# Part of a depthwise convolution moved from VectorE to TensorE, four rows to a product in four column tiles

## The chip, the cores and the metric

The kernel runs on one core of a Trainium2 chip. The metric is the device time of the whole program in microseconds (us); before the change its median over three runs is 2747.23 us (2745.68 to 2749.08). The engines are called as in the profile: PE is TensorE's matmul, PEld its weight load, DVE VectorE, ACT ScalarE, POOL GpSimd, SP SyncE (it issues transfers only).

## The reference

The input is x, 4 images of 384 channels of 48 x 48 float32. For each image:

```python
x_flat = x.reshape(B, C, N).transpose(0, 2, 1)              # N = 48*48 = 2304 tokens
local = conv(x, conv_w, 7x7, padding='SAME', groups=C)      # depthwise: each channel by itself
local = local * inv + (bn_beta - bn_mean * inv)             # batch norm, inv = gamma*rsqrt(var+eps)
x_norm = layernorm(x_flat)                                  # over the 384 channels
q, k, v = x_norm @ qkv_w.T + qkv_b                          # 8 heads of 48
q = q + layernorm(local_flat)                               # the convolution joins the query
out = softmax(q @ k.T * 48**-0.5) @ v
return x_flat + (out @ proj_w.T + proj_b)                   # back to NCHW
```

The convolution has 49 taps a channel, and every output token needs it before its query is whole.

## The kernel before

**Tiling.** The 384 channels lie as CC = 3 chunks of 128 partitions, in an order that packs head pairs. An image's tokens are cut in two ways. For layer norm, keys and values there are NG = 6 groups of 384 tokens (8 image rows), g = 0 to 5. For the convolution, queries and attention there are NA = 5 groups a image, of ROWS = 8, 10, 10, 10, 10 image rows, so 384 or 480 tokens; over the four images they are numbered t = 0 to 19.

**The convolution.** `load_slab` brings a group's rows with three rows above and below into a slab, on the POOL queue. `conv_ops(t)` is a generator that yields one tap of one chunk at a time: one DVE instruction (L331) that multiplies the shifted window of the slab by the tap's weight (`cw`, one per channel) and adds it to `accs[t]`. The weights contain the batch norm's factor, and the first tap adds its shift: for t = 0 on DVE (L327), for all later groups on ACT in `first_taps` (L295). `taps` are sorted by the distance of their row, then of their column, from the middle. All generators are chained into one `stream`; `convolve_first(n)` takes n taps of it in the start stage, `convolve(point)` a planned number later.

**What TensorE does of it.** Only ten taps (`PE_TAPS`) of chunk 0 of group t = 0: `make_diagonals` builds ten diagonal matrices on ACT (L340), `products` multiplies the shifted windows by them into one PSUM bank (L347), and `add_products` adds that bank to the accumulator on DVE (L1088). The order of t = 0 is therefore: chunks 1 and 2 tap by tap in turn, and then the 39 left taps of chunk 0 alone.

**The start stage** (0 to 159 us) normalizes image 0 and makes its keys and values, group by group, in an order written out by hand for each engine. `from_x(0, g)` is a generator of pairs of projections, `both(making)` runs one pair: its products on PE and then its evacuations on ACT. For a group g the order is: values 0 and 1; the mean of the next group's x (`mean_by_chunk`, three products of 128 x 384 against a matrix of 1/384; a float32 product is two PE instructions); 7 taps; `centre` on DVE (L536) and squares on ACT; value 2 and key 0; 6 taps; the sum of squares over the three chunks (two DVE adds, `sum_squares`, L493 and L494) and its mean (`mean_in_place`, one product, L526); keys 1 and 2; the root on ACT; the first key's low half (`lows_out`, L731); queries 0 and 1; 9 taps; two more low halves; two DVE steps of Newton and the scaling of the next x (L616); query 2; 7 taps. The values of group g + 1 need that scaled x. For g = 5 the group's convolved rows t = 0 are normalized in place of a next x, and become queries (`local_end`, `query_end`, `low_queries`).

**Attention.** A group t has twelve slots, s = 0 to 11 (four head pairs, three batches of six blocks of 128 keys). A slot is 36 score products (L1032), six exponentials on ACT (L1040) and 24 instructions of weighing (L1047). Beside them DVE does taps and the norm of the next group: `norm.sum` of its accumulator (L493, L494), `mean_of_sum`, `centre`, squares, `mean_kept`, root, `local_end`, `query_end`, `low_queries`. In t = 0 these stand at slots 8 to 10. `low_queries` makes the queries' low half on DVE (L900) and then moves rows within SBUF by six transfers (L905, L907), three on SP and three on another queue; the first scores need all of them.

**Between images** a stage with points ("kv", t, g, h) makes the next image's keys and values and the last image's output projection; its residual sums are `finish` (L1013), which free the PSUM bank they read.

**The planner.** `spare` and `spare_at_keys` give, in us, the DVE time that is free at each point, less the costs of what else is done there; `due` says by which point each group's convolution must be whole; `plan` spreads the taps over the points at the least rate that meets all due points, and `share` holds the result.

Of the kernel before, what the change touches and what calls it, by code (L numbers as in the profile page):

```python
# [10 lines left out]
F32 = mybir.dt.float32  # L11
HALF = mybir.dt.float32r
AF = mybir.ActivationFunctionType
# [15 lines left out]
X_LATER = 3  # L29
OUT_SLOT = 7  # L30
WARM = 14
PE_TAPS = 10
AHEAD = 18
FIRST_ROOM = 4.0

# [13 lines left out]
def unshifted_pass(  # L49
# [40 lines left out]
    def columns_of(t):  # L90
        return size(tokens[t % NA])
# [14 lines left out]
    def two_banks(name="r"):  # L106
        return ps.tile([P, 2, 512], F32, tag="r", name=name)
# [121 lines left out]
    def pack():  # L229
# [18 lines left out]
    diagonals = [  # L248
        work.tile([P, 2, GM], F32, tag="pt", name="pt", bufs=4) for _ in range(-(-PE_TAPS // 6))
    ]  # L250
    staged = [
        work.tile([P, CC, GM], F32, tag="qs", name="staged", bufs=5)[:, :, :C] for _ in range(3)
# [48 lines left out]
    def conv_ops(t):  # L301
        b, g = divmod(t, NA)
        if t + 1 < NT:
            load_slab(*divmod(t + 1, NA))
        slab, first, end = slabs[b, g]
        if t == 0:
            begin_sums(t)
            nc.vector.memset(accs[0][:, 0, :], 0.0)
        while soon:
            soon.popleft()()  # L310
        acc = accs[t]

        order = [(tap, c) for tap in taps for c in range(CC)]
        if t == 0:
            order = [o for o in order if o[1]] + [(tap, 0) for tap in taps[PE_TAPS:]]
        for i, (tap, c) in enumerate(order):
            if i == len(order) - AHEAD and t + 1 < NT:
                begin_sums(t + 1)
                soon.append(lambda: first_taps(t + 1))
            part = window(slab, acc[:, c, :], g, first, end, c, tap)  # L320
            if not part:
                continue
            src, dst = part
            weight = cw[:, c, tap : tap + 1]
            if tap == taps[0]:
                if t == 0:
                    nc.vector.tensor_scalar(  # L327
                        dst, src, weight, shift[:, c : c + 1], ALU.mult, ALU.add
                    )
            else:  # L330
                nc.vector.scalar_tensor_tensor(dst, src, weight, dst, ALU.mult, ALU.add)  # L331
            if t == 0 or tap != taps[0]:
                yield

    def diagonal(i):
        return diagonals[i // 6].rearrange("p i f -> p (i f)")[:, i % 6 * P : i % 6 * P + P]

    def make_diagonals():
        for i in range(PE_TAPS):
            nc.scalar.mul(diagonal(i), ident, cw[:, 0, taps[i] : taps[i] + 1])  # L340

    def products():
        total = two_banks()[:, 0, : columns_of(0)]
        slab, first, end = slabs[0, 0]
        for i, tap in enumerate(taps[:PE_TAPS]):
            src, part = window(slab, total, 0, first, end, 0, tap)
            nc.tensor.matmul(  # L347
                part, lhsT=diagonal(i), rhs=src, start=i == 0, stop=i == PE_TAPS - 1
            )
        return total  # L350

# [65 lines left out]
    weights = [0.0]  # L417
    for t in range(1, NT):
        last = ("slot", t - 1, norm_slots(t - 1)[0] - (t >= NA), t < NA) if t % NA else ("kv", t, 4, 0)
        counts.append(t * (each - CC))  # L420
# [665 lines left out]
    def add_products():  # L1086
        a = accs[0][:, 0, :]
        nc.vector.scalar_tensor_tensor(a, first_sum, shift[:, 0:1], a, ALU.add, ALU.add)  # L1088


    def warm(n):
        m = two_banks()[:, 0, 0:P]
# [51 lines left out]
    norm.scale(norm.newton())  # L1144
    both(making)
    convolve_first(7)
    for g in range(1, NG):

        last = g == NG - 1
        making = from_x(0, g)  # L1150
        both(making)
        if last:
            added = output_bias()
        else:
            norm = Norm(xn[0, g + 1])
            norm.mean_by_chunk(norm.src)
            convolve_first(7)
        if g in (3, 5):
            keep_stack(0, g // 2 - 1)
        norm.centre()  # L1160
        norm.squares()
        if last:
            convolve_first(6)
        both(making)
        if last:
            norm.mean_by_chunk(norm.buf)
        else:
            convolve_first(6)
            norm.sum_squares()
            both(making)  # L1170
            norm.mean_in_place()
        norm.root()
        if last:
            convolve_first(9)
            local_end(0, norm.newton())
            query_end(0, True)
            both(making)
            low_queries(0, 0, nc.scalar)
            convolve_first(2)
            lows_out(1)  # L1180
            both(making)
            convolve_first(4)
            both(making)
            continue
        lows_out(1)
        both(making)
        convolve_first(9)
        lows_out(2)
        norm.scale(norm.newton())
        both(making)  # L1190
        if g == NG - 2:
            assert n_first >= each - PE_TAPS
# [5 lines left out]
    made = n_first - (each - PE_TAPS)  # L1198
    plan(made)
    convolve("start")  # L1200

    for t in range(NT):
        b, g = divmod(t, NA)
        if g == 0 and b:
# [4 lines left out]
            for gk in range(NG):  # L1209
# [727 lines left out]
```

## Time and profile before

| what | value |
|---|---|
| median of three runs | 2747.23 us |
| the profiled execution | 2748.89 us |
| its span, first to last instruction | 2747.0 us |
| mean granted TensorE clock | 0.997 |
| convolution on DVE (L331), 2871 instructions | 1685.9 us busy |
| scores (L1032) and weighing (L1047) on PE | 969.9 and 1167.5 us busy |
| projections and means on PE (L621), groups of w_qk, w_v and w_o | 283.7, 147.0 and 85.2 us busy |
| start stage, to the first score | 158.88 us |
| attention of t = 0, first score to first score of t = 1 | 158.88 to 259.31 us |

The shares of busy time say that PE is nearly always busy, but a matmul's end is modelled, so they do not say that it runs at its pace. The pace is read from the starts: equal slots follow each other at 9.07 us with 480 tokens and at 7.38 us with 384, and a slot that takes longer has lost time. The busy times by 20 us (us from the span's start, then each engine's busy time and number of instructions, granted clock, DMA share, GB/s) show where PE has gaps:

```profile
core 0: us, PE busy (x) PEld busy (x) DVE busy (x) ACT busy (x) POOL busy (x), PEclk, DMA share, GB/s
100.00:120.00 20.00, 17.59 (x50) 9.79 (x49) 18.98 (x35) 8.47 (x16) 12.32 (x25) 0.91 0.36 79
200.00:220.00 20.00, 18.75 (x144) 11.18 (x144) 20.00 (x34) 14.02 (x21) 1.45 (x2) 1.00 0.46 141
220.00:240.00 20.00, 17.12 (x128) 10.27 (x125) 19.97 (x33) 11.80 (x18) 4.38 (x7) 1.00 0.74 184
```

In these stretches PE has gaps while DVE has almost none, and in the first the granted clock falls as well.

### The profile page before, as it was taken

The numbers are of one execution on the slowest core, as the hardware profiler recorded it, in microseconds if no ns is written. First come the engines' busy times: TensorE is split into PE (matmuls) and PEld (weight loads), VectorE is DVE, ScalarE is ACT, GpSimd is POOL, SyncE is SP. The second block draws the span as 40 slices with busy tenths as digits, with TensorE's granted clock in tenths as the row PEclk, the third lists the DMA queues.
The fourth block names the chain that finished last, engine by engine and source line by source line (L and its number), as shares of the span: only waits on it lengthen the run. The fifth ranks groups of instructions, "written<-read, shape, count | busy, mean of one in ns | idle before, by whom it ended". The sixth has DMA issues, their size and how long they took to land.

```text
span 2747.0 us, 45879 instructions
## 1 busy us (share of the span) xinstructions
PE 2718.1 (99%) x16358; PEld 1538.0 (56%) x16358; DVE 2334.3 (85%) x4065; ACT 1672.2 (61%) x2319; POOL 600.4 (22%) x1073
## 2 busy tenths in 40 slices
PE   8999999999999999999999999999999999999999
PEld 5565555555565655555555655555555565555555
DVE  7999999989898999988889999889788888986212
ACT  4356777777335767777622667777752376766662
POOL 4541101112453111011155211111225501110110
PEclk9999999999999999999999999999999999999999
DMA  7454544446355445354555553545635545444442
GB/s 142 96 151 116 137 120 127 132 129 182 99 151 154 134 132 137 122 148 124 149 137 135 163 154 107 140 127 142 148 108 159 144 138 133 138 132 126 143 144 76
DMA packets 159710, 369.10 MB, mean 134 GB/s; under 512 B 58416, under 2 KB 107600, under 8 KB 159472
## 3 DMA queue, kind: packets, MB, share of 16 engines
q0 software_dynamic: 71232, 278.45, 35.2%
q1 hardware_dynamic: 82496, 77.13, 12.4%
q10 hardware_dynamic: 5744, 10.50, 1.2%
q8 instruction: 132, 2.16, 0.3%
q14 instruction: 106, 0.87, 0.1%
HBM read 258.14 MB, written 64.14 MB: 117 GB/s over the span
## 4 chain that ended last, share of the span: by engine, by line
PE 82%; DVE 12%; DMA 4%; issue 1%; ACT 1%; SPq 0%; POOL 0%; DVEq 0%; ACTq 0%; POOLq 0%
PE o L1047 39%; PE r L1032 32%; PE r L621 11%; DVE acc L331 7%; DMA four<-parts 1%; DMA parts<-part 1%; DVE k L731 1%; DMA qs<-qs 0%; DVE xr L1013 0%; DMA wide<-k 0%; DVE xn L616 0%; DVE xn L881 0%; DVE acc L869 0%; DMA pb<-in_proj_b_dram 0%; DMA qk_vec<-in_qk_b_dram 0%
## 5 line engine op out<-in xcount | busy, mean ns | idle before, releaser
L331 DVE SCALAR_TENSOR_TENSOR acc<-slab,vec,acc 128x470 f32<-128x470 f32 (+9 forms) x2871 | 1685.9, 657 | 1.3
L1040 ACT ACTIVATE pt<-r 128x960 f32<-128x960 f32 (+1 forms) x1440 | 1248.4, 942 | 248.8 <-PE o L1047 157.2
L1047 PE MATMUL o<-pt,v 128*64 128x480 f32 (+1 forms) x5760 | 1167.5, 555 | 0.4 <-ACT pt L1040 0.4
L1032 PE MATMUL r<-qs,ks 64*128 64x480 f32 (+1 forms) x8640 | 969.9, 374 | 7.6 <-DVE xr L1013 4.1
L1032 PEld LDWEIGHTS r<-qs,ks 64*128 64x128 f32 x8640 | 784.8, 184 | 274.6 <-issue 173.7
L1047 PEld LDWEIGHTS o<-pt,v 128*64 128x64 f32 x5760 | 392.8, 137 | 661.2 <-issue 568.6
L693 POOL DMA_DIRECT2D ks<-wide x220 | 159.8, 726 | 1363.4 <-PE r L1032 1286.3
L621 PE MATMUL r<-xn,w_qk 128*128 128x384 f32 x864 | 283.7, 486 | 0.0
L924 ACT COPY o<-o 113x480 f32<-113x480 f32 (+1 forms) x160 | 87.1, 544 | 286.3 <-PE o L1047 286.2
L621 PEld LDWEIGHTS r<-xn,w_qk 128*128 128x128 f32 x864 | 164.2, 190 | 114.5
L621 PE MATMUL r<-w_v,xn 128*128 128x384 f32 x432 | 147.0, 493 | 3.8 <-DVE xn L616 2.4
L715 ACT COPY v<-r 128x384 f32<-128x384 f32 x72 | 32.1, 480 | 190.7 <-PE r L621 190.7
L943 DVE TENSOR_TENSOR ao<-ao,o 113x480 f32<-113x480 f32 (+1 forms) x120 | 75.8, 632 | 78.8 <-ACT o L924 78.6
L621 PEld LDWEIGHTS r<-w_v,xn 128*128 128x128 f32 x432 | 82.1, 192 | 64.1 <-issue 4.7
L900 DVE TENSOR_TENSOR qs<-xn,qs 128x480 fp32r<-128x480 f32 (+1 forms) x60 | 38.0, 633 | 70.7 <-ACT qs L895 70.7
L678 POOL DMA_DIRECT2D wide<-k x144 | 72.1, 503 | 95.3 <-ACT k L728 82.0
L621 PE MATMUL r<-af,w_o 128*128 128x384 f32 (+1 forms) x270 | 85.2, 470 | 0.0
L943 DVE TENSOR_TENSOR aot<-aot,o 113x480 f32<-113x480 f32 (+1 forms) x40 | 25.3, 632 | 65.0 <-ACT o L924 64.9
L114 POOL DMA_DIRECT2D slab<-in_x_dram x76 | 41.9, 558 | 145.7 <-DVE acc L331 142.4
L745 ACT ACTIVATE xn<-r,qkb 128x384 f32<-128x384 f32 x72 | 39.4, 578 | 55.5 <-PE r L621 40.6
L934 ACT COPY ao<-o 113x480 f32<-113x480 f32 (+1 forms) x60 | 32.6, 543 | 64.5 <-PE o L1047 64.5
L728 ACT ACTIVATE k<-r,qkb 128x384 fp32r<-128x384 f32 x72 | 39.4, 581 | 52.7 <-PE r L621 39.7
(143 smaller groups left out, 1355.5 us busy)
## 6 DMA issues: line engine op xcount, KB each, us to landing
ks<-wide POOLq DMA_DIRECT2D x220, 768.0 KB, 5.0
qs<-qs SPq DMA_DIRECT2D x352, 60.0 KB
slab<-in_x_dram POOLq DMA_DIRECT2D x24, 432.0 KB, 7.5
wide<-k POOLq DMA_DIRECT2D x96, 96.0 KB, 2.3
wide<-ks POOLq DMA_DIRECT2D x12, 768.0 KB, 4.3
xr<-in_x_dram POOLq DMA_DIRECT2D x16, 576.0 KB, 5.3
rb<-rden SPq DMA_DIRECT2D x32, 270.0 KB
held<-ao POOLq DMA_DIRECT2D x12, 720.0 KB, 3.9
```

The lines of the kernel that those rows point to most:

```text
L114: queue.dma_start(out=dst[p0 : p0 + piece.shape[0]], in_=piece)
L331: nc.vector.scalar_tensor_tensor(dst, src, weight, dst, ALU.mult, ALU.add)
L621: nc.tensor.matmul(dst, lhsT=weights(c), rhs=src(c), start=c == 0, stop=c == CC - 1)
L678: nc.gpsimd.dma_start(out=last[16 * u : 16 * u + 16, 0], in_=k[r : r + 16, 0])
L693: queue.dma_start(out=place_keys(b, p, i), in_=wide[b, p][:, :, at])
L728: nc.scalar.activation(k[:, 0, :], r[:, :G], AF.Identity, bias=bias)
L745: nc.scalar.activation(src[:, i, :], q[:, :G], AF.Identity, bias=qkb[:, 0, i : i + 1])
L924: nc.scalar.copy(part[0 : 64 + HA], sums[0 : 64 + HA, 0, :n])
L943: nc.vector.tensor_add(dst, dst, part[0 : 64 + HA])
L1032: nc.tensor.matmul(r[:, j, :n], lhsT=ks[rows, w, at], rhs=qs[rows, m, :], start=i == 0, stop=i == 2,)
L1040: nc.scalar.activation(pt, r[:, :, :n], AF.Exp, scale=SCALE)
L1047: nc.tensor.matmul(sums[halves[j], 0, : columns_of(t)], lhsT=values[t // NA, kb // NB][:, first : first + 64], rhs=pt[:, j, :], start=i == ...
```

## The change

Chunk 0 of the second group (t = 1, 480 tokens) is convolved by TensorE alone; DVE does chunks 1 and 2 of it (96 taps). All three chunks of t = 0 are DVE's, in turn (147 taps); the diagonals and their sum are gone.

- `copies_in` makes four tiles by 16 transfers on SP. Tile q holds the 32 channels of quarter q four times, on partitions 0 to 31, 32 to 63 and so on, each copy shifted by one more image row. A column of such a tile holds four rows of a channel, so one product of 128 rows does four taps of one column offset (dy = 0 to 3); a second one with 96 rows does the other three (dy = 4 to 6, `a` = 1).
- `spread_out` and `taps_out` make the weights: for each quarter, column offset and `a`, a matrix of 128 (or 96) x 32 with the taps of each channel on four (three) small diagonals. Four products choose the quarters' taps, seven ACT copies put them in place, and two DVE multiplies of 128 x 896 and 96 x 896 spread them.
- `products` runs 7 column offsets x 2 x 4 quarters = 56 products into one bank, each quarter in its own column tile of 32 output partitions. One ACT instruction adds the shift and writes the chunk of `accs[1]`.
- The means of the x of groups 2 to 5 are made as one product from the sum of the three chunks, two DVE adds at the end of the group before (`norm.sum`, `mean_in_place`), in place of three products.
- The counts of `convolve_first` change: 22 a group in place of 29 and 24 more in group 2, where `products` stands; 179 taps before attention in place of 183.
- `spare_at_keys` takes 1.5 and 3.0 us off the points (5, 3) and (5, 4); the queries' transfers between images are all put on SP.

```diff
-PE_TAPS = 10
+SHIFTS = 4
...
-        for c in range(CC):
+        for c in range(t == 1, CC):
             src, dst = window(slab, accs[t][:, c, :], g, first, end, c, taps[0])
...
-            begin_sums(t)
-            nc.vector.memset(accs[0][:, 0, :], 0.0)
+            begin_sums(0)
+            begin_sums(1)
...
-        if t == 0:
-            order = [o for o in order if o[1]] + [(tap, 0) for tap in taps[PE_TAPS:]]
+        if t == 1:
+            order = [o for o in order if o[1]]
...
+    def copies_in():
+
+        slab, first, end = slabs[0, 1]
+        slab = slab[:, 0].rearrange("p (h w) -> p h w", w=W)
+        for q, rows in enumerate(quarters):
+            for i, to in enumerate(quarters):
+                n = min(rows_kept, end - first - i)
+                nc.sync.dma_start(out=copy_of(q)[to, 0:n], in_=slab[rows, i : i + n])
...
+    def taps_out():
+        m = two_banks()[:, 0, 0 : 4 * T0].rearrange("p (q v) -> p q v", q=4)
+        for q in range(4):
+            nc.tensor.matmul(
+                m[:, q, :],
+                lhsT=chosen[:, q * P : (q + 1) * P],
+                rhs=cw[:, 0, :],
+                start=True,
+                stop=True,
+            )
+        for i, rows in enumerate(quarters):
+            for a in range(2):
+                dy = a * SHIFTS + i
+                if dy < KS:
+                    nc.scalar.copy(few_taps[rows, a], m[rows, :, dy * KS : (dy + 1) * KS])
+        for a in range(2):
+            k, dst = taps_of(a)
+            w = few_taps[0:k, a].rearrange("p q d -> p (q d)")
+            nc.vector.tensor_tensor(
+                dst[0:k],
+                same_row[0:k].rearrange("p (o j) -> p o j", o=1).to_broadcast([k, 28, 32]),
+                w.rearrange("p (i o) -> p i o", o=1).to_broadcast([k, 28, 32]),
+                ALU.mult,
+            )
 
     def products():
-        total = two_banks()[:, 0, : columns_of(0)]
-        slab, first, end = slabs[0, 0]
-        for i, tap in enumerate(taps[:PE_TAPS]):
-            src, part = window(slab, total, 0, first, end, 0, tap)
-            nc.tensor.matmul(
-                part, lhsT=diagonal(i), rhs=src, start=i == 0, stop=i == PE_TAPS - 1
-            )
-        return total
+        total = two_banks()[:, 0, : columns_of(1)]
+        order = sorted(range(KS), key=lambda d: abs(d - PAD))
+        todo = [(a, d) for d in order for a in range(2)]
+        n = ROWS[1]
+        for a, d in todo:
+            k, w = taps_of(a)
+            dx = d - PAD
+            c0, c1 = max(0, -dx), min(W, W - dx)
+            for q, rows in enumerate(quarters):
+                nc.tensor.matmul(
+                    total[rows].rearrange("p (h w) -> p h w", w=W)[:, :, c0:c1],
+                    lhsT=w[0:k, q * KS + d, :],
+                    rhs=copy_of(q)[0:k, a * SHIFTS : a * SHIFTS + n, c0 + dx : c1 + dx],
+                    start=(a, d) == todo[0],
+                    stop=(a, d) == todo[-1],
+                )
+        nc.scalar.activation(accs[1][:, 0, :], total, AF.Identity, bias=shift[:, 0:1])
...
-            (5, 1): 4.5, (5, 2): 0.6,
+            (5, 1): 4.5, (5, 2): 0.6, (5, 3): 1.5, (5, 4): 3.0,
...
-    make_diagonals()
+    copies_in()
+    spread_out()
...
-    first_sum = products()
...
-    add_products()
...
+    norm = Norm(xn[0, 2])
+    norm.sum()
     for g in range(1, NG):
...
-            norm = Norm(xn[0, g + 1])
-            norm.mean_by_chunk(norm.src)
-            convolve_first(7)
+            norm.mean_in_place()
+            convolve_first(6)
...
-            convolve_first(6)
+            if g == 1:
+                taps_out()
+            if g == 2:
+                products()
+                convolve_first(24)
+            convolve_first(5)
             norm.sum_squares()
...
-        convolve_first(9)
+        convolve_first(6)
...
-        convolve_first(7)
+        convolve_first(5)
+        if g < NG - 2:
+            norm = Norm(xn[0, g + 2])
+            norm.sum()
...
-                    low_queries(t, 0, nc.scalar)
+                    low_queries(t, 0)
```

More of the change, by code (lines that the diff above doesn't have):

```diff
@@ L247, in unshifted_pass @@
     w_o = const.tile([P, CC, C], F32, tag="w_o", name="w_o")
-    diagonals = [
-        work.tile([P, 2, GM], F32, tag="pt", name="pt", bufs=4) for _ in range(-(-PE_TAPS // 6))
+    spread_taps = [
+        work.tile([P, CC, GM], F32, tag="ao", name="spread").rearrange("p c n -> p (c n)")
+        for _ in range(2)
+    ]
+    copies = [
+        work.tile([P, CC, GM], F32, tag="qs", name="copies", bufs=5).rearrange("p c n -> p (c n)")
+        for _ in range(2)
     ]
@@ L313, in conv_ops @@
         order = [(tap, c) for tap in taps for c in range(CC)]
-        if t == 0:
-            order = [o for o in order if o[1]] + [(tap, 0) for tap in taps[PE_TAPS:]]
+        if t == 1:
+            order = [o for o in order if o[1]]
         for i, (tap, c) in enumerate(order):
             if i == len(order) - AHEAD and t + 1 < NT:
-                begin_sums(t + 1)
+                if t:
+                    begin_sums(t + 1)
                 soon.append(lambda: first_taps(t + 1))
@@ L333, in conv_ops @@
                 yield
[L335 to L340, printed above, removed]
-    def products():
-        total = two_banks()[:, 0, : columns_of(0)]
-        slab, first, end = slabs[0, 0]
-        for i, tap in enumerate(taps[:PE_TAPS]):
-            src, part = window(slab, total, 0, first, end, 0, tap)
-            nc.tensor.matmul(
-                part, lhsT=diagonal(i), rhs=src, start=i == 0, stop=i == PE_TAPS - 1
-            )
-        return total
+    quarters = [slice(32 * i, 32 * i + 32) for i in range(4)]
@@ new lines, in unshifted_pass, with copy_of @@
+    few_taps = piece(2, 4, KS)
+    same_row = piece(32)
+    chosen = spread_taps[0][:, 2 * 448 : 2 * 448 + 512]
+    rows_kept = max(ROWS) + SHIFTS
+    def copy_of(q):
+        n = rows_kept * W
+        return copies[q // 2][:, q % 2 * n : (q % 2 + 1) * n].rearrange("p (h w) -> p h w", w=W)
+    def copies_in():
[5 more added lines that the diff above has]
+                nc.sync.dma_start(out=copy_of(q)[to, 0:n], in_=slab[rows, i : i + n])
@@ new lines, in taps_of, with spread_out @@
+    def taps_of(a):
+        k = P - 32 * (a * SHIFTS + SHIFTS - KS)  if a else P
+        return k, spread_taps[a][:, 0:896].rearrange("p (i j) -> p i j", j=32)
+    def spread_out():
+        each_four = chosen.rearrange("p (q i j) -> p q i j", q=4, i=4)
+        nc.scalar.copy(
+            each_four,
+            ident.rearrange("p (q o j) -> p q o j", q=4, o=1).to_broadcast([P, 4, 4, 32]),
+        )
+        nc.vector.tensor_reduce(
+            same_row, ident.rearrange("p (i j) -> p j i", j=32), AX.X, ALU.add
+        )
@@ new lines, in taps_out @@
+    def taps_out():
[21 more added lines that the diff above has]
+                ALU.mult,
+            )
@@ new lines, in products @@
+    def products():
+        total = two_banks()[:, 0, : columns_of(1)]
[13 more added lines that the diff above has]
+                    stop=(a, d) == todo[-1],
+                )
+        nc.scalar.activation(accs[1][:, 0, :], total, AF.Identity, bias=shift[:, 0:1])
@@ L419, in unshifted_pass @@
         last = ("slot", t - 1, norm_slots(t - 1)[0] - (t >= NA), t < NA) if t % NA else ("kv", t, 4, 0)
-        counts.append(t * (each - CC))
+        counts.append(counts[-1] + (each - CC if t > 1 else (CC - 1) * (KS * KS - 1)))
         weights.append(weights[-1] + (counts[-1] - counts[-2]) * columns_of(t) / G)
@@ L1084, in convolve_first @@
             next(stream)
-    def add_products():
-        a = accs[0][:, 0, :]
-        nc.vector.scalar_tensor_tensor(a, first_sum, shift[:, 0:1], a, ALU.add, ALU.add)
     def warm(n):
@@ L1191, in unshifted_pass @@
         if g == NG - 2:
-            assert n_first >= each - PE_TAPS
+            assert n_first >= each
             norm = Norm(accs[0])
             norm.mean_by_chunk(norm.src)
-        convolve_first(7)
+        convolve_first(5)
+        if g < NG - 2:
+            norm = Norm(xn[0, g + 2])
+            norm.sum()
     lows_out(2)
     nc.vector.tensor_add(pb, pb, added)
-    made = n_first - (each - PE_TAPS)
+    made = n_first - each
     plan(made)
```

## The prediction

> **What bounds the kernel now.** I read the page first (busy shares, then the chain that ended last), then who TensorE (PE) waited for over the whole span, then the timeline around each of those waits.
>
> ```profile
> PE 2718.1 (99%) x16358; PEld 1538.0 (56%) x16358; DVE 2334.3 (85%) x4065; ACT 1672.2 (61%) x2319; POOL 600.4 (22%) x1073
> ...
> PE 82%; DVE 12%; DMA 4%; issue 1%; ACT 1%; SPq 0%; POOL 0%; DVEq 0%; ACTq 0%; POOLq 0%
> ```
>
> PE bounds the span; VectorE (DVE) owns 12% of the chain. So a change can gain in two ways: fewer PE instructions, or DVE earlier where PE waits for it. PE's own waits, in total us, times, longest:
>
> ```profile
> PE r L1032 <- DVE xr L1013: 4.1, 2, 2.1
> ...
> PE r L621 <- ACT sq L488: 2.9, 1, 2.9
> PE r L621 <- DVE xn L616: 2.4, 1, 2.4
> ```
>
> Each starts with DVE being late. The timeline shows that each costs more than its wait. Prices in the start stage (start, us, line, shape, count):
>
> ```profile
> 23.10 2.33 PE L795 MATMUL r<-staged,of_ln 128*1 128x384 f32 x18 [1.74 <-issue]
> 29.34 6.29 PE L347 MATMUL r<-slab,pt 128*128 128x384 f32 x20
> 74.33 2.10 PE L621 MATMUL r<-xn,mean_w 128*128 128x384 f32 x6
> 113.02 5.83 PE L621 MATMUL r<-w_v,xn 128*128 128x384 f32 x12 [2.41 <-DVE xn L616]
> ```
>
> A float32 product is two instructions. Groups 1, 2 and 3 start their values at 50.46, 70.46 and 90.45: 20.0 us for 62 instructions of 384 columns, 0.3225 us each. The twelve at 113.02, after PE had sat idle 2.41 us, took 0.49 each: half clock for a while, another 2 us. L795 is the row most like the new products: three column tiles (output partitions 0, 32, 64), 18 instructions whose starts lie between 23.1 and 25.0. One after the other they would need 18 x 0.3225 = 5.8 us; in 2.33 us all three tiles must have run at once.
>
> DVE's taps:
>
> ```profile
> 20.71 14.08 DVE L331 SCALAR_TENSOR_TENSOR acc<-slab,vec,acc 128x376 f32<-128x376 f32 x28
> 89.41 8.43 DVE L331 SCALAR_TENSOR_TENSOR acc<-slab,vec,acc 128x360 f32<-128x360 f32 x14
> ```
>
> 28 taps that alternate between two chunks take 0.50 each. From 89.92 to 118.5 DVE works off the leftover taps of chunk 0 alone, each adding to what the one before wrote: 14 take 0.60 each, though their windows are no larger. A step in the critical chain at 90.51 reads 0.62.
>
> The first attention group (t=0) and an image boundary:
>
> ```profile
> 206.07 3.04 PE L1032 MATMUL r<-qs,ks 64*128 64x384 f32 x31 [1.25 <-DMA qs<-qs]
> ...
> 236.90 1.65 DVE L536 TENSOR_TENSOR acc<-acc,sq 128x1440 f32<-128x1440 f32 x1
> ...
> 239.24 4.21 PE L621 MATMUL r<-sq,mean_w 128*128 128x480 f32 x6 [2.88 <-ACT sq L488]
> ```
> ```profile
> 845.32 3.76 DVE L331 SCALAR_TENSOR_TENSOR acc<-slab,vec,acc 128x450 f32<-128x450 f32 x6
> ...
> 849.00 1.34 DVE L1013 SCALAR_TENSOR_TENSOR xr<-r,pb,xr 128x480 f32<-128x480 f32 x2
> ...
> 850.39 1.61 PE L1032 MATMUL r<-qs,ks 64*128 64x384 f32 x12 [2.01 <-DVE xr L1013]
> ...
> 851.92 5.42 PE L1047 MATMUL o<-pt,v 128*64 128x384 f32 x24
> ```
>
> An undisturbed slot of 384 columns lasts 7.38 us (scores start at 167.14, 174.51, 181.90). Against that, slot 6 of t=0 is 1.65 late (204.03 to 213.06), and slots 9 and 10 start 14.47 apart (228.91, 243.38) where slot and mean need 7.38 + 2.42: 4.7 lost. At the boundary six taps of point ("kv", 5, 5, 4) stand ahead of the two residual sums that free a PSUM bank; the slot lasts 11.42, so 4.0 are lost. The same point costs 3.9 at 2178.56 and 0.5 at 1513.56.
>
> [...]
>
> **The change, part by part.**
>
> *PE, start stage.* Gone: 20 instructions of L347, 6.3 us, and 4 of 6 instructions in four first means, 16 x 0.3225 = 5.2. New: 14 tap steps x 4 tiles x 2 = 112 instructions. With four tiles at once that is 28 steps; the windows average 463 of 480 columns, 0.3225 x 463/384 = 0.389, so 10.9, and 0.5 to fill: 11.4. Bounds: 10.9 below; 43.6 if no tiles overlap. I take 11.4 because L795 shows three whole tiles at once. The four selecting products of taps_out are 8 instructions of 49 columns; pack (L234) took 1.66 for 14, so 1.0. Net +0.9.
>
> *DVE, start stage.* Taps before attention fall from 183 to 179. All three chunks of the first group now alternate: 147 taps at a mean of 0.467 by their windows are 68.6. Before, 98 at that price and 39 dependent at 0.575 were 68.2: ten more taps for nothing. Of the second group 32 taps stand where 46 did: 14 x 0.61 = 8.5 less. Memset and add_products: 0.9 less. Added: eight adds of first sums at 0.59 (L493 and L494 cost that) = 4.7; two multiplies of 128x896, about 1.05 each by L536's 1.35 for 1152; the identity's sum 0.3. Net about -2.
>
> *Order decides what that is worth.* Without L347, PE reaches the mean of xn 1 about 6 us sooner, but the centring waits behind 31 taps on DVE; that chain gains only the 1.9 us in which DVE idled at 36.67 and add_products, and PE idles some 3 us, with half clock likely. Group 1 starts 1 to 3 us earlier; I take 2. In group 1 the two multiplies stand on DVE right after the centring, and need PE (the values, then the selecting products) and seven small ACT copies (0.2 each, by L861 and L810): DVE waits about 3 us, with five taps, the sum of squares and the key's low half queued behind it, and PE's next mean waits for that sum. Group 2 then starts 1.9 later than before. Group 2 takes 58 x 0.3225 + 11.4 = 30.1 on PE; its 24 extra taps (11 to 13 us) lie beside the products: +11.9 at its end. Groups 3 and 4 have 58 instructions, 18.7 us each, and DVE (22 taps at 0.43 and 8 us of norm work, 17.7) no longer falls behind, so the stall at 113.02 with its half clock goes. Group 5's values start 4.6 later; but what ended before there was DVE's centring of accs[0] at 140.81, behind 7 taps; with those gone it waits for its mean and starts at about 141.9. The first score is **1.1 us later** (bounds -4 to +6 with four tiles).
>
> *Other engines.* The 16 copies go on SP after w_o: 16 x 0.6 issue, from 39.3 to about 50; the key stacking that began at 39.98 comes up to 10 us later, which nobody reads before attention, and its key buffer returns at about 62. ACT loses ten L340 (3.0) and gains copies: nothing on the path.
>
> *t=0.* Following plan's arithmetic with the new counts, its slots get 123 taps instead of 131; up to the centring at 236.90 seven fewer, 4.3 us. The squares then come just as PE needs them, so PE never idles long enough to lose clock: of 4.7 + 1.65 I expect **-6.0**. Slots 0 and 11, late by their transfers, stay as they are.
>
> *t=1, t=2.* Ten taps fewer in each. The mean at 445.36 waited 0.8, and the slot after 455.41 is 0.8 long by late squares: **-1.3**.
>
> *Boundaries.* The new costs take point (5, 4) from 6 or 5 taps to 0 and (5, 3) from 5 to 3. The residual sums then end before PE wants the bank: 4.0 + 0.5 + 3.9 = -8.4. low_queries puts six transfers on SP instead of three each on SP and ACT: at 840.26, six issues of 0.7 and some 2.2 to land give 846.7, and PE is ready at 845.9; about 0.7, 0 and 0.9 at the three. Net **-6.9**. SP's key stacking moves 2 us later, with 15 us in hand.
>
> *Elsewhere* the taps come back as one or two more per later group; PE keeps its 9.07 us slot there while DVE has room, so nothing.
>
> Sum: 1.1 - 6.0 - 1.3 - 6.9 = -13.1. The profiled execution took 2748.89 (span 2747.0 and 1.9 around it); it lies 1.7 above the median 2747.23. So 2734.
>
> **Rivals.**
> - *The start stage is dearer* (0.20). Three tiles at once give 37 steps, +3.6; two give 56, +10.9; half clock after the idle in group 0 or 1 adds about 2. For: four were never seen, and 8 loads must fit into 0.39 us. Against: L795. Result 2738 to 2745.
> - *The transfers eat the boundaries' gain* (0.08). The transfers issued at 255.99 took 5.3 us to land; with that instead of 2.2 each boundary loses 3 us: 2743. Against: the boundary is not loading keys.
> - *Slower: the column tiles run one after the other* (0.12). 112 x 0.389 = 43.6 instead of 10.9, in group 2, where nothing covers it, for DVE has only 24 taps to do: 2767. It decides from a products stage of 25 us. For: the fourth tile, with changing row counts (128 and 96), is unseen. Against: L795, and the two tiles of L1047 (24 instructions in 4.09, 0.34 per pair).
> - *Better* (0.12): DVE's relief wins in the start stage too, no wait in group 1, no half clock: 4 to 6 us more, 2729.
>
> **How the numbers follow.** The forecast has 0.48: 2734, its own range 2729 to 2739. With the better case, the dearer start and the transfers, 2725 to 2745 leaves out the serial tiles and a little at the edges. A measurement can tell 0.2%, 5.5 us, from no change. Below 2741.7 lie the forecast, the better case, three quarters of the dearer start and a little of the transfers: 0.78. Slower is the serial case, 0.12; the rest 0.10.
>
> **What would show it.** Products of about 11.5 us in group 2; taps of group 3 at 0.47; no wait of PE at L621 in group 4; the first score near 160; slots 9 and 10 of t=0 about 10 apart; boundary slots of 7.4 to 8.3. The forecast is wrong if the products take over 15 us, if PE idles over 2 us twice in groups 0 to 2, or if the slots' stalls stay.

## The result, and the profile after

The changed kernel takes 2740.54 us (median of 14 runs, 2736.99 to 2743.9); the kernel before, run beside it, 2746.26 us (14 runs, 2742.41 to 2750.27). The ratio is 0.9979 (95% interval 0.9971 to 0.9987): 5.7 us faster, where 13.1 were forecast. (The ratios in this document are the recorded ones, from runs side by side; they are not quotients of the medians.)

The profiled execution of the changed kernel took 2736.99 us. It is the fastest of its 14 runs, while the profiled one of the kernel before, 2748.89, lies near the upper end of its own. The two profiles therefore differ by 11.9 us, twice what the medians do. So both kernels were profiled a second time (the first two experiments). The table puts the four executions side by side, in us, by stages that are read from the starts of the score products (the attention of t = 4, 9 and 14 ends 9.07 us after the start of its last slot, and the boundary's row begins there):

| stage | before | before, second | change | change, second | forecast of the difference |
|---|---|---|---|---|---|
| start stage, to the first score | 158.9 | 158.6 | 161.0 | 165.2 | +1.1 |
| t = 0 | 100.4 | 100.6 | 94.6 | 94.6 | -6.0 |
| t = 1 to 4 | 445.2 | 445.5 | 444.0 | 443.8 | -1.3 |
| first boundary, t = 5 to 9 | 669.6 | 668.9 | 667.4 | 668.6 | |
| second boundary, t = 10 to 14 | 664.3 | 664.3 | 663.7 | 663.7 | |
| third boundary, the rest | 708.6 | 707.4 | 704.3 | 704.3 | -6.9 for all three |

The t = 0 to 4 rows are as forecast in both pairs. The start stage and the boundaries are not settled by one pair: the start is 2.2 or 6.7 us longer, the boundaries are 7.0 or 3.9 us shorter.

The page of the changed kernel, busy shares and the chain that ended last:

```profile
PE 2715.1 (99%) x16442; PEld 1536.5 (56%) x16442; DVE 2313.1 (85%) x4036; ACT 1671.0 (61%) x2317; POOL 599.5 (22%) x1073
...
PE 89%; DVE 8%; DMA 2%; ACT 1%; SPq 0%; issue 0%; POOL 0%; DVEq 0%; ACTq 0%
```

Compared with before, DVE has 29 instructions and 21 us less to do, and its share of the chain falls from 12% to 8%. PE has 84 instructions more and yet 3 us less of busy time. What PE waited for (total us, times, longest):

```profile
PE r L593 <- DVE sq L561: 2.7, 1, 2.7
...
PE r L688 <- ACT sq L550: 2.5, 1, 2.5
```

Of the waits shown of before (residual sums, scaled x, squares of slot 9) none is over 0.5 us now. Two new ones stand in the start stage. Its PE timeline (start, us, line, shape, count, idle before and its releaser):

```profile
39.34 2.20 PE L688 MATMUL r<-sq,mean_w 128*128 128x384 f32 x6 [2.48 <-ACT sq L550]
...
63.17 0.88 PE L593 MATMUL r<-sq,mean_w 128*128 128x384 f32 x2 [2.68 <-DVE sq L561]
...
78.78 11.11 PE L410 MATMUL r<-copies,spread 128*32 128x480 f32 x112
...
100.24 4.03 PE L688 MATMUL r<-w_v,xn 128*128 128x384 f32 x12
...
118.95 4.03 PE L688 MATMUL r<-w_v,xn 128*128 128x384 f32 x12
...
137.66 2.10 PE L688 MATMUL r<-acc,mean_w 128*128 128x384 f32 x6
```

The 112 instructions of the products take 11.11 us, 0.397 for each of the 28 steps of four, where one product of their mean length is 0.389 by the prediction's estimate: all four column tiles run at once. Groups 3 and 4 last 18.7 us each, and the stall at 113 is gone. The two waits are the first and the second line: group 0's mean waits for squares, group 1's for a sum that DVE makes late. Why late, DVE's timeline shows:

```profile
57.59 2.09 DVE L393 TENSOR_TENSOR spread<-start_up 128x896 f32<-128x896 f32 x2 [2.98 <-ACT start_up L389]
...
62.47 0.56 DVE L561 TENSOR_TENSOR sq<-sq 128x384 f32<-128x384 f32 x1
```

DVE idles 2.98 us for the weights' ACT copies, and the five taps and the two sums for PE's mean (the second of them is the last line) are queued behind.

The end of the stage, from the values of group 5 to the first score, decides the forecast's first term. The busy times of it, before and after, and the centring of t = 0, which the prediction takes as the limit there:

```profile
137.04:158.88 21.84, 21.53 (x80) 13.26 (x78) 21.73 (x35) 6.92 (x14) 11.20 (x22) 1.00 0.36 94
139.59:161.04 21.45, 21.45 (x79) 13.23 (x77) 18.41 (x30) 7.12 (x14) 9.30 (x18) 1.00 0.43 108
...
140.81 1.34 DVE L536 TENSOR_TENSOR acc<-acc,r 128x1152 f32<-128x1152 f32 x1
...
139.79 1.35 DVE L603 TENSOR_TENSOR acc<-acc,r 128x1152 f32<-128x1152 f32 x1
```

The first line of each pair is before, the second the change. The centring comes 1.0 us earlier and the first score still 2.2 us later: PE works through this stretch without a gap (before, with one of 0.31 us), so its own products set the length. The columns of the first pair are those of the busy times below and before.

The busy times by 20 us, in two of the stretches shown of before (the same columns):

```profile
100.00:120.00 20.00, 20.00 (x64) 11.79 (x63) 18.57 (x37) 8.52 (x16) 14.16 (x29) 1.00 0.41 92
...
220.00:240.00 20.00, 19.48 (x136) 11.24 (x134) 19.97 (x32) 12.49 (x20) 1.45 (x2) 1.00 0.33 113
```

PE fills these stretches now, at full clock (1.00, in the first 0.91 before); in the last of them its gaps fall from 2.88 to 0.52 us. In t = 0, slots 9 and 10 start 10.58 apart (229.15, 239.73) instead of 14.47.

### The profile page after: what moved, and what is told of

It is laid out like the page before. It is cut to its first block, busy times and chain, and to the rows that moved or that the text cites. A ratio compares the mean times of both kernels' runs of the same rounds, so it can differ in the third digit from the quotient of the medians.

```text
span 2735.1 us, 46034 instructions
## 1 busy us (share of the span) xinstructions
PE 2715.1 (99%) x16442; PEld 1536.5 (56%) x16442; DVE 2313.1 (85%) x4036; ACT 1671.0 (61%) x2317; POOL 599.5 (22%) x1073
## 4 chain that ended last, share of the span: by engine, by line
PE 89%; DVE 8%; DMA 2%; ACT 1%; SPq 0%; issue 0%; POOL 0%; DVEq 0%; ACTq 0%
PE o L1114 37%; PE r L1099 31%; PE r L688 20%; DVE acc L337 6%; DMA xn<-in_x_dram 1%; DMA rd<-den 0%; PE r L410 0%; DMA qs<-qs 0%; DMA slab<-in_x_dram 0%; SPq L974 0%; DVE acc L936 0%; DVE xn L948 0%; DMA staged<-in_qkv_wT_dram 0%; PE r L587 0%; DVE ao L1010 0%
## 5 line engine op out<-in xcount | busy, mean ns | idle before, releaser
L337 DVE SCALAR_TENSOR_TENSOR acc<-slab,vec,acc 128x470 f32<-128x470 f32 (+10 forms) x2832 | 1657.9, 656 | 4.2 <-ACT acc L300 4.2
L745 POOL DMA_DIRECT2D wide<-k x144 | 72.0, 502 | 100.4 <-ACT k L795 76.5
L795 ACT ACTIVATE k<-r,qkb 128x384 fp32r<-128x384 f32 x72 | 39.3, 580 | 53.5 <-PE r L688 39.1
L1080 DVE SCALAR_TENSOR_TENSOR xr<-r,pb,xr 128x384 f32<-128x384 f32 (+2 forms) x72 | 41.9, 611 | 34.0 <-PE r L688 25.2
```

The lines of the kernel that those rows point to most:

```text
L745: nc.gpsimd.dma_start(out=last[16 * u : 16 * u + 16, 0], in_=k[r : r + 16, 0])
L795: nc.scalar.activation(k[:, 0, :], r[:, :G], AF.Identity, bias=bias)
L1080: nc.vector.scalar_tensor_tensor(xr[:, co, :], m, pb[:, co : co + 1], xr[:, co, :], ALU.add, ALU.add)
```

## The experiments

Ten more runs were made, two of them of the same two kernels. The medians of before that stand beside them are 2746.36 (41 runs, the first four), 2746.2 (22, the next four) and 2745.79 us (9, the last two).

**The same two kernels again** (no edit).

> The changed kernel once more, for a second profile. Theory A (half clock by luck): the stalls stand where they stood (groups 0 and 1 about 2.5 us each, score start near 161), but the number of half-clock windows of 3.4 us differs from the one of the first profile, 2 to 4, each costing 1.7 us, and the time is near 2740.5. Theory B (the moved taps cost time later): the slots of the later groups lose 3 us or more against their 9.07 and 7.38 us in this profile again, at the same places (group 6, slots at 993 to 1031 us).

> The kernel before once more, for a second profile. Theory A: the same stalls (113, 239, 850, 2182 us), but fewer than the four half-clock windows of the first profile, 2 or 3; time near 2746.3, ratio 1.000. Theory C (the stalls themselves come and go): some of the stalls at the image boundaries, 4.0 and 3.9 us in the first profile, are gone or under 1 us.

Measured: the change 2741.05 us, ratio 0.9973 (0.9963 to 0.9984); before 2746.86, 1.0001 (0.9993 to 1.0009). The stages are in the table above. Theory A came true for the change: the two waits stand where they stood, and the time lost to half clock differs. Before has half clock at three of its four stalls (at the first of them the twelve instructions from 112.70 take 5.83 us again), and the third boundary's stall is 2.45 us instead of 3.9. The later slots of the change lose 2.1 us at two places of t = 6, under theory B's 3. In the second profile of the change the first score is at 165.2, with the same work in the same order. Its PE timeline:

```profile
39.57 4.21 PE L688 MATMUL r<-sq,mean_w 128*128 128x384 f32 x6 [3.07 <-ACT sq L550]
...
66.41 1.62 PE L593 MATMUL r<-sq,mean_w 128*128 128x384 f32 x2 [2.68 <-DVE sq L561]
```

The waits are nearly those of the first profile, 3.07 and 2.68 us (2.48 and 2.68 there). But the mean after the first takes 4.21 us for six instructions instead of 2.20, and that after the second 1.62 for two instead of 0.88: the clock is granted at a half (0.50 from 40 to 44 us). By the trace's clock record each such stretch lasts 3.4 us (here 6.8 from 38.8 on, and 3.4 from 66.1), so each costs PE up to half of that, 1.7 us. One execution has them and another, with nearly the same waits, has none: three times 1.7, so 5.1 us, is as much as the two spans differ by (2735.1 and 2740.3).

The twelve traces show what it goes with. In each, all half-clock stretches begin on one grid with a step of 3.413 us: in the first profile of before at 113.96, 240.25, 851.24 and 2182.44 us, so 37, 179 and 390 steps apart, in `after_no_spare` at 16.67, 40.57, 64.46 and 849.52 us, so 7, 7 and 230. Against the program this grid lies differently in every execution. PE's idle time can be counted within each step (after the first 20 us of a span, ends of products as modelled). All 20 steps with 1.99 us or more of it were followed by half clock, two of the five with 1.70 to 1.86, and one of the 21 with 1.0 to 1.6. The wait of 2.68 us in group 1, step by step, in the first profile of the change and in the second (busy times as above; PEclk is the third number from the right):

```profile
58.89:62.30 3.41, 1.61 (x5) 0.59 (x4) 3.41 (x7) 1.05 (x2) 0.90 (x2) 1.00 0.00 0
62.30:65.72 3.42, 2.55 (x8) 1.63 (x9) 3.39 (x8) 1.56 (x3) 3.42 (x8) 1.00 0.41 109
...
62.73:66.14 3.41, 1.00 (x4) 0.25 (x2) 3.38 (x8) 1.05 (x2) 1.50 (x4) 1.00 0.08 22
66.14:69.56 3.42, 3.15 (x5) 1.85 (x6) 3.42 (x8) 1.43 (x3) 3.42 (x7) 0.50 0.45 118
```

In the first a step's edge cuts it into 1.80 and 0.87 us, and no clock is lost. In the second 2.41 us of it lie in one step, and the next is at half clock. The wait of group 0 was cut into 1.55 and 0.93 in the first profile. By this reading the first profile had neither stretch because of where the grid lay. It is read from the traces; no run moves the grid by intent.

**The two planner costs alone, and all but them.** `after_no_spare` takes the two numbers out of the change, `before_spare` puts them alone into the kernel before:

```diff
-            (5, 1): 4.5, (5, 2): 0.6, (5, 3): 1.5, (5, 4): 3.0,
+            (5, 1): 4.5, (5, 2): 0.6,
```

> The change without the two new planner costs (1.5 and 3.0 at points (5,3) and (5,4)). If the boundaries gain what the first profile showed (9 us), this is 8 to 9 us slower than the changed kernel, so 2 to 3 us slower than before; if they gain only the idle time without the half clock, 4 to 6 us slower; boundary slots of 11 us again at two of three boundaries.

> The kernel before with only the two new planner costs. Mirror of the run without them: 8 us faster than before if the profile's boundaries are typical (ratio 0.997), 4 to 6 us faster under theory A (0.998); all three boundary slots near 7.4 to 7.8 us. Start stage and t = 0 as before (first score 159, slots 9 and 10 14 us apart).

Measured: the change without them 2744.89 us, 0.9995 (0.9988 to 1.0001); before with them alone 2740.8, 0.9976 (0.9967 to 0.9986). Both differences are those of the smaller forecasts, 4 to 6 us. So two numbers in the planner are worth as much as the whole change: with them the moved convolution gains 0.3 us (2740.8 to 2740.54), without them 1.5, and neither is clear of the noise. In the trace of `after_no_spare` the residual sums are late again, in the waits:

```profile
PE r L1099 <- DVE xr L1080: 3.9, 2, 2.7
```

and the first slot of t = 5 is 6.5 us late, where the change has 1.7; half clock from 849.5 on is a part of it (the 24 weighing instructions from 849.42 take 5.79 us, at full clock 4.09). In the medians the two costs are worth 4.4 us within the change (2744.89 - 2740.54) and 5.6 in the kernel before (2746.36 - 2740.8). The forecast had 8.4 for them, before 1.6 given back.

**Unread products in the two waits** of the start stage. They remove no wait; they only keep PE at work: eight products of 128 x 128 in group 0, nine in group 1, into the unused second bank of the mean's PSUM pair. The text of both edits is alike:

```diff
-            self.m = two_banks()[:, 0, : self.n]
+            r = two_banks()
+            self.m = r[:, 0, : self.n]
+            for _ in range(fill):
+                nc.tensor.matmul(r[:, 1, 0:P], lhsT=mean_w, rhs=ident, start=True, stop=True)
...
-    norm.mean_by_chunk(norm.buf)
+    norm.mean_by_chunk(norm.buf, fill=8)
...
-            norm.mean_in_place()
+            norm.mean_in_place(9 if g == 1 else 0)
```

> The changed kernel with 8 and 9 products of 128x128 that nobody reads, put where PE waits in groups 0 and 1 of the start stage (2.5 to 3.1 and 2.7 us), 1.75 and 2.0 us of work. Theory A (the start stage is dear because these waits cost half-clock windows of 3.4 us, 1.7 us each): no half-clock window at 39 to 68 us, group 1's mean at full pace (0.81 us), first score near 161, 2.5 to 3.5 us faster than the changed kernel (ratio to before near 0.9967). Rival (the waits themselves are the cost, or the filling delays the means): first score stays at 163.5 to 165, time unchanged or 1 us more.

Measured: 2736.45 us, 0.9957 (0.9944 to 0.9971), 4.1 us less than the change. The PE timeline:

```profile
36.02 1.95 PE L574 MATMUL r<-ident,mean_w 128*128 128x128 f32 x16
39.57 2.20 PE L694 MATMUL r<-sq,mean_w 128*128 128x384 f32 x6 [1.60 <-ACT sq L550]
...
60.56 2.17 PE L598 MATMUL r<-ident,mean_w 128*128 128x128 f32 x18
63.40 0.88 PE L599 MATMUL r<-sq,mean_w 128*128 128x384 f32 x2 [0.67 <-DVE sq L561]
```

Both means start where they started without the fill (39.3 and 63.2), at full pace (2.20 us for six instructions and 0.88 for two, granted clock 1.00), and the first score is at 161.3. The work that counts begins no earlier than in the change's first profile (161.0), which lost no clock here. So the gain is lost clock. Its size is less sure than its cause: 4.1 us between the medians, with only 5 runs of this kernel; 2.3 between this first score and the mean of four profiles of the change's own start (163.6, below). Two stretches are 3.4.

**The selecting products early.** The four selecting products and the seven ACT copies move from group 1 into PE's wait in group 0; the two DVE multiplies stay in group 1, as `taps_spread`. Two taps move with it, so that the sum stays 179:

```diff
     both(making)
+    taps_out()
     convolve_first(2)
     norm.mean_by_chunk(norm.buf)
...
-                taps_out()
+                taps_spread()
...
-            convolve_first(5)
+            convolve_first({1: 3, 3: 6, 4: 6}.get(g, 5))
```

> The changed kernel with the selecting products and their seven copies moved to group 0's wait, and two taps moved from group 1 to groups 3 and 4. DVE finds the weights ready: its 3.0 us wait in group 1 goes and PE's 2.7 us wait there falls under 1 us. Theory A: 1.9 us less wait and no half-clock window at 64 to 68 us, the first score 3 to 4 us earlier, 3 us faster. Rival (DVE's work, not its wait, sets group 1): PE waits 2 us or more at the same place and less than 1 us is won.

Measured: 2734.39 us, 0.9953 (0.9939 to 0.9967), 6.2 less than the change. The PE timeline:

```profile
36.73 0.99 PE L378 MATMUL r<-vec,spread 128*128 128x49 f32 x8
39.15 2.20 PE L690 MATMUL r<-sq,mean_w 128*128 128x384 f32 x6 [1.43 <-ACT sq L552]
...
59.77 0.81 PE L595 MATMUL r<-sq,mean_w 128*128 128x384 f32 x2
```

The wait of group 1 is gone (its mean has no idle before it and comes 3.4 us earlier), that of group 0 falls to 1.43 us, and no clock is lost in these groups (1.00 granted from 36 to 68 us). The first score is at 157.0, earlier than before's 158.9 by 1.9. Two taps fewer in group 1 are about 1 us of this. This is what the change's start could have been.

**The queries' transfers on two queues again**, as before the change:

```diff
-                    low_queries(t, 0)
+                    low_queries(t, 0, nc.scalar)
```

> The changed kernel with the queries' transfers between images on SP and ACT again. The first slot of group 5 was 1.7 and 2.0 us late in two profiles; if the single queue is the cause (six issues and landing after PE is ready), it is under 0.7 us late here and the run 1 to 1.5 us faster; if PE waits there for something else, it stays near 1.8.

Measured: 2741.47 us, 0.9977 (0.9968 to 0.9987): nothing gained. The lateness of 1.7 at the first boundary's first slot is gone, but the stage ahead of it takes 144.3 us instead of 139.5, with a wait that the change doesn't have:

```profile
PE r L688 <- DVE k L798: 2.6, 1, 2.6
```

and a half-clock stretch at 843.6 (the 12 instructions from there take 6.76 us, six of the same shape before them 2.58). The same wait (2.54), half clock after it (6.77 for the 12) and a similarly longer stage (145.7) stand in `before_spare`, which also has both queues and the new costs. Both traces are of the slowest of their ten executions, so this wait need not be in a typical one. By the medians two queues gain nothing over one. Whether the wait comes of both together, and why, was not tried.

**Unread products in the stall of t = 0**, in the kernel before: ten of them ahead of the mean at slot 9.

```diff
-            m = two_banks()[:, 0, : self.n]
+            r = two_banks()
+            m = r[:, 0, : self.n]
+            for _ in range(10):
+                nc.tensor.matmul(r[:, 1, 0:P], lhsT=mean_w, rhs=ident, start=True, stop=True)
```

> The kernel before with 10 unread products of 128x128 (2.2 us) put where PE waits for the squares at slot 9 of t = 0 (2.9 us). Theory A: no half-clock window near 240 us; slots 9 and 10 are 1.7 us closer (12.7 instead of 14.4 apart) and the run 1.7 us faster (ratio 0.9994). Rival (clock is no part of the loss): 14.4 apart as before, ratio 1.000.

Measured: 2743.61 us, 0.9992 (0.9984 to 1.0). The PE timeline:

```profile
235.87 2.50 PE L516 MATMUL r<-ident,mean_w 128*128 128x128 f32 x20
239.09 2.68 PE L624 MATMUL r<-sq,mean_w 128*128 128x480 f32 x6 [0.72 <-ACT sq L488]
```

The mean takes 2.68 us where it took 4.21, t = 0 98.9 instead of 100.5. So in the traces 1.6 of the 5.9 us that the change saves in t = 0 were clock; of the rest about 1.7 is slot 6, late by 1.65 and 1.82 in the two profiles of before and on time in the change, and the others are the late squares themselves. The interval of the medians reaches 1.0 and does not show it by itself.

**Two versions of the early selection.** `early_filled` adds four unread products in what is left of group 0's wait; `early_softer` takes a third off the two planner costs.

```diff
-    norm.mean_by_chunk(norm.buf)
+    norm.mean_by_chunk(norm.buf, fill=4)
```

```diff
-            (5, 1): 4.5, (5, 2): 0.6, (5, 3): 1.5, (5, 4): 3.0,
+            (5, 1): 4.5, (5, 2): 0.6, (5, 3): 1.0, (5, 4): 2.0,
```

> The change with the selecting products early, plus four unread 128 x 128 products (about 1 us) in the PE wait of group 0 that is left, 1.43 us. Theory (idle gaps of 2 to 3 us are what costs half clock, shorter ones do not): a gap of 1.4 us trips nothing, so filling it moves nothing: first score 157.0 +-0.5, median 2734 +-1.5, no half-clock stretch in groups 0 to 2 in either. Rival (shorter gaps trip it too in part of the executions): the filled one is 1 to 2 us faster, median 2732.5.

> The change with the selecting products early, and the two planner costs at 1.0 and 2.0 us in place of 1.5 and 3.0. Theory (the taps that leave the image boundaries come back as late slots of t = 6 and a late slot 48, some 3 us in all): fewer taps return there, slots 79 and 82 are under 0.4 late each, while the boundaries lose 1 to 2 us more than with the full costs: median 2732 to 2735. Rival (the late slots of t = 6 do not come from the boundary costs): they stay at 0.8 to 1.0 and the boundaries lose 2 to 4 us more: median 2736 to 2738.

Measured: 2733.68 us, 0.9956 (0.9943 to 0.997), and 2734.06, 0.9958 (0.9944 to 0.9971): both the same as `after_early_taps` within the noise. The first expectation failed in its mechanism. In the trace of `early_filled` the unread products waited themselves, for DVE's centring (L608), which reads the mean before it from PSUM:

```profile
39.15 1.13 PE L576 MATMUL r<-ident,mean_w 128*128 128x128 f32 x8 [1.99 <-DVE xn L608]
40.25 3.89 PE L693 MATMUL r<-sq,mean_w 128*128 128x384 f32 x6
```

They stood behind the wait, not in it, and this execution lost clock from 40.35 on (0.66 granted from 39 to 44 us). And in that of `early_softer` 1.70 us were enough (0.57 granted from 39 to 43 us), all of them in one step of the grid:

```profile
38.99 3.89 PE L690 MATMUL r<-sq,mean_w 128*128 128x384 f32 x6 [1.70 <-ACT sq L552]
```

Of the second expectation the sizes came (slots 79 and 82, counted through all groups, no longer late; the first slot of t = 5 is 2.5 late instead of 0.6), but not the reason: `early_filled`, with the full costs, has no late slots 79 and 82 either, and its first slot of t = 5 is 1.6 late; in `after_filled` neither is late, and that first slot is 3.5 late. What decides where DVE's arrears of this stretch are paid stays open.

## Why the prediction was right or wrong

**Right, with its sizes.** The products: 11.4 forecast, 11.11 measured, four tiles at once, against a rival of 43.6. PE's waits in group 0 and 1, "some 3" and "about 3 us" of DVE: 2.48 to 3.07, and 2.98. Group 2: 30.1 forecast, 30.05 measured (70.19 to 100.24). Groups 3 and 4 at 18.7, without the stall. Chunk 0's taps alternate: 28 of them in 13.27 us, 0.474 each, where 14 took 0.60. t = 0: -6.0, measured -5.8 and -6.0. t = 1 to 4: -1.3, measured -1.2 and -1.7.

**The step that failed** is the end of the start stage, on which "The first score is **1.1 us later**" rests. The prediction let group 5's values start 4.6 later, and then took 3.5 of this off again, because "what ended before there was DVE's centring of accs[0] at 140.81". It was not. The centring came at 139.79 in the first profile, 1.0 earlier than before, and the first score 2.2 later. PE sets this stretch: from the values of group 5 to the first score it takes 21.45 us in all eight profiles with the moved convolution, without any idle time, where before took 21.8 in its two. Only 0.4 could be gained there, not 3.5. With its own 4.6 this term should have read 4.2.

Up to group 5 the sum was near. Four profiled executions have the change's own start: the two of the change, `after_no_spare` and `after_two_queues`. Against the mean of the two profiles of before, group 1's values start 1.3 earlier on average (forecast 2), group 2's 2.5 later (1.9), group 3's 12.5 (11.9), group 5's 5.3 (4.6). The first score is at 163.6 on average (161.0, 165.2, 163.6, 164.5), 4.9 later. Lost clock decides where in this range an execution lies (none in these groups at 161.0, three times 3.4 us of half clock at 165.2). The prediction wrote "half clock likely" for group 0, took 2 out of "1 to 3" there, and priced it fully only in a rival. In the first profile, which lost no clock here, groups 1 to 5 start 1.3 to 2.2 earlier than forecast (against the first profile of before), so the sum had room for about that much lost clock, though no term of it says so. `after_filled` shows that it costs: PE kept busy in these waits, and nothing else changed, gives 4.1 us between the medians. The prediction's own sign of being wrong, PE idle over 2 us twice in groups 0 to 2, came.

**A second term was too large**: the boundaries, -6.9. Their three stalls (4.0, 0.5, 3.9) were taken from one execution, in which two of the waits were followed by half clock (at 851.2 and 2182.4). In the second profile of before only the first was, and the third boundary's stall was 2.45 instead of 3.9. By the medians the two planner costs are worth 4.4 within the change, with the single queue already in. The first boundary also keeps a late slot (1.7 to 2.0, forecast 0.7), and slots 79 and 82 of t = 6 are late by 1.8 together, which the prediction's "Elsewhere ... nothing" left out. The sum of the parts is a slip besides: 8.4 less 0.7 and 0.9 is 6.8, not 6.9.

**A third is the base.** The sum was taken off one execution, 2748.89, which is 2.6 above the median that the kernel before showed beside the change. For a kernel whose executions differ by how many waits lost clock, the stalls of one execution aren't those of the median one. A rough balance of the second pair of profiles: +6.7 (start) - 6.0 - 1.7 - 3.9 = -4.9; the medians give -5.7.

**The rivals.** The dearer start happened in its half-clock part, and the median lies in its 2738 to 2745, outside the forecast's own 2729 to 2739; its two or three tiles at a time did not. That the number lies there is in part luck, since PE's work at the end of the stage, the larger cause, was in no rival. (Its "8 loads must fit into 0.39 us" should be 4: 112 instructions in 28 steps.) The serial tiles did not happen. The transfers did not eat the boundaries: two queues are no better. The better case, "no wait in group 1, no half clock", is what `after_early_taps` builds.

**What is shown and what not.** That the waits' lost clock costs the change time is shown by the fill, its size (2.3 to 4.1 us) less exactly. That the wait in group 1 comes from the ACT copies is shown by moving them; the two taps that moved along, about 1 us, cannot make a wait of 2.68. That PE sets the end of the stage is read from eight traces, not from an edit. Why one wait of 2.7 us loses clock and another doesn't is read from the grid of the stretches, whose step is 3.413 us in these traces; no experiment sets it. 1.99 us of idle time or more within one step always led to half clock here (20 of 20), so less idle time than a whole step is enough; what decides it at 1.70 to 1.86 us (two of five) is not shown.

## What to carry to other kernels

Before an earlier release on a side engine is counted as a gain, look whether the bounding engine has a gap to close there: at the end of this start stage it had none. A wait of TensorE can have a second price, the slower clock after it (here half clock for 3.41 us, so up to 1.7 us), and it is paid in a share of the executions (here after nine of twelve waits of 2.41 to 3.07 us): put the wait down with that price as soon as the profile shows one like it, and fill it with work from elsewhere in the order (here the selecting products) before counting the gain. Take a stall's size from several executions, and test small constants of a planner by themselves, for they can be worth as much as the large change they come with. When a step is moved onto another engine, the waits between its small parts can cost more than their work (here DVE waits 2.98 us for seven copies that keep ACT busy for 0.94).

## What the runs showed of the hardware

- Within the program half-clock stretches (0.50 granted) last 3.41 us or twice that, begin on a grid of 3.413 us whose place differs from execution to execution, and follow steps in which PE idles much: 20 of 20 steps with 1.99 us or more, two of five with 1.70 to 1.86, one of 21 with 1.0 to 1.6. So a wait shorter than a step can lose clock (1.70 us did in `early_softer`), and the same wait loses it or not: the waits of 2.41 to 3.07 us in groups 0 and 1 of the change's start and in before's group 4 did in nine of twelve cases, in eight executions.
- Four column tiles of 32 columns with 128 or 96 rows and float32 run at once: 28 steps of four in 11.11 us, 0.397 each. A plain instruction of 384 columns takes 0.3225; by length, one of 463, the average here, would take 0.389 (an estimate).
- DVE's taps that add to what the one before wrote cost 0.60 us (14 taps from 89.41 on, before, windows of 346 columns on average). When accumulators alternate they cost 0.474 (28 taps from 77.80 on, the change, 328 columns) to 0.50.
